# Graph attention on one core: 40 columns of x a group on ScalarE, 12 a group on VectorE

## The chip, the cores and the metric

The kernel runs on one core of a Trainium2 chip. The metric is device time in microseconds (us) for one execution; smaller is better. The engines are named as in the profile: PE (TensorE, with PEld for its weight loads), DVE (VectorE), ACT (ScalarE), POOL (GpSimd) and SP (SyncE). A "q" behind a name (DVEq, ACTq) is that engine's sequencer: register operations, loads of registers and waits on semaphores, which do not count as busy time of the engine.

## The reference

A graph attention layer over N = 12500 nodes and 212500 edges sorted by destination, with D = 128 and 8 heads of 16:

```python
Q, K, V = x @ WQ, x @ WK, x @ WV              # [N, 8, 16] each
Eh = edge_attr @ WE                           # [E, 8, 16]
score = K[src] * Q[dst] / 4 * Eh
score = exp(clip(score.sum(-1, keepdims=True), -5, 5))
wV = segment_sum(V[src] * score, dst)
Z = segment_sum(score, dst)
h = x + wV / (Z + 1e-6)
h = (h - mean(h)) * rsqrt(var(h) + 1e-5) * gamma + beta   # over the nodes
out = layernorm(x + h)                                    # over the features
```

All data are f32. The sources of the edges are random, so K[src] and V[src] have to be fetched row by row.

## The kernel before

The edges are cut into 1661 tiles of 128. Two units of four tiles make a group, and there are 208 groups of eight tiles (the last is smaller). First a table of K and V of all nodes, `kvd`, is made in DRAM (256 f32 a row). Then one long loop goes over the groups. For each tile of a group 128 rows of the table are wanted; an indirect DMA on POOL (`gather`, L272) brings them, one DMA a tile, into the group's buffer `slot`. There are eight such buffers and a ninth from group 6 on, so gathers can run some groups ahead of their use.

Within the loop, group g goes through these steps on DVE, in this order: `products` (L755, twice: K times the product of Q and Eh, which lies in `ps_t`), `scores` (L762, the sum in each head), `clip_exp` (L771 on DVE, then two exponentials on ACT, L772 and L773), `recip`, `turned_onehot`, `both_halves` (L732), `attn` (L809), `message` (L777: V times the exponential), `onehot` for group g+1 (L674, L676, L677). PE makes the products with matrices, the sum over the edges (L793) and the turns; ACT evacuates PSUM.

POOL's gathers are saved in three ways for some groups, which the code calls `apart`: their eighth tile is not gathered by POOL.

- By columns on ACT: `hx` holds x transposed in SBUF (128 x N). `load_cols` reads node numbers into ACT's registers (`TENSOR_LOAD`, L326, from `col_ids`), and `fetch_cols` copies one column of `hx` a time into `xc` (L363), 32 a group, 16 ahead of the exponentials (half 0) and 16 behind them (half 1). When 128 columns stand, `cols_mm` (L371, on PE) multiplies them with `w_kv` into `pair_ps`, and `cols_out` (L375, on ACT) puts the 256 results into the group's `slot`. `col_plan` says which groups: 49 tiles.
- By rows on SP: `fetch_rows` issues 16 DMAs of one row each a group into `byrow`; `rows_out` (L353, on ACT) copies 128 of them into `slot`. `row_plan`: 24 tiles.

The exponentials and `pair_ps` share one PSUM tile, `ps_m`. The order on each engine is that of the code (the schedule is written out by hand), and a gather is also tied to steps of the loop (`pace`).

The loop's middle, in the order of the code before:

```python
fetch_rows(g)
within(products, g); within(denom, g - 2); within(scores, g)
fetch_cols(g, 0)
within(clip_exp, g); within(recip, g - 2); within(turned_onehot, g + 2); within(both_halves, g + 1)
...
within(gather_sum, g - 1); within(eh_mm, g + 2); cols_mm(g); fetch_cols(g, 1)
within(x_out, g - 3); within(q_out, g + 3); within(sums_out, g - 1)
cols_out(g); rows_out(g)
within(eh_out, g + 2); within(q_window, g + 4); load_cols(g + 1)
within(turn_back, g + 1); within(qe_mm, g + 2)
within(attn, g - 2); within(message, g); within(onehot, g + 1)
```

Of the kernel before, what the change touches and what calls it, by code (L numbers as in the profile page):

```python
# [21 lines left out]
G = 8  # L22
U = 4
# [22 lines left out]

LAST = [3, 2]
# [27 lines left out]
def col_plan(sizes):  # L75
    full = sizes.count(U) // 2
    groups, end = [], P
    while FIRST_COL + -(-end // COLS) - 1 + COL_LAG < full:
        groups.append(max(NX, FIRST_COL + -(-end // COLS) - 1 + COL_LAG))
        end += P  # L80
    assert sorted(set(groups)) == groups
    return groups


def row_plan(sizes):
    full, used = sizes.count(U) // 2, set(col_plan(sizes))
    groups, end = [], P
    while True:
        g = FIRST_ROW + -(-end // SP_ROWS) + ROW_LAG
        while g in used:  # L90
            g += 1
        if g >= full:
            return groups
        used.add(g)
        groups.append(g)
        end += P


def row_groups(sizes):
    return [2 * g for g in col_plan(sizes) + row_plan(sizes)]  # L100


@with_exitstack
def gnn_kernel(
# [31 lines left out]
    consts = ctx.enter_context(tc.tile_pool(name="consts", bufs=1))  # L136
# [23 lines left out]
    pair_ps = small_ps[:, 0:2, :].rearrange("p a b -> p (a b)")  # L160
# [91 lines left out]
    KV, XG, SLOT, PAIR = {}, {}, {}, {}  # L252
# [30 lines left out]
    def issue(n=0):  # L283
        while len(queued) > n:
            f, *a = queued.pop(0)
            f(*a)
# [9 lines left out]

    col_tiles = col_plan(usizes)
    tot = len(col_tiles) * P
    assert tot % (2 * COLS) == 0 and tot // (2 * COLS) <= P and P % COLS == COLS % LOAD == 0
# [4 lines left out]
    apart = set(col_tiles + row_tiles)  # L304
    row_ids = consts.tile([P, 2 * SP_ROWS], I32, name="row_ids")
    nc.vector.memset(row_ids, 0)
    rows_in = [tc.alloc_semaphore(f"rows_in{i}") for i in range(NSEM)]
    kvb = kvd.bitcast(U8).rearrange("n d -> (n d)")
    BY_ROW = {}
    XC = {}  # L310

    def load_col_ids():
        n, m = 2 * SP_ROWS, tot_rows // (2 * SP_ROWS)
        nc.sync.dma_start(row_ids[:m], bass.AP(tensor=rsrc.tensor, offset=rsrc.offset + tot, ap=[[n, m], [1, n]]))
        m = tot // (2 * COLS)
        nc.sync.dma_start(col_ids[:m], bass.AP(tensor=rsrc.tensor, offset=rsrc.offset, ap=[[2 * COLS, m], [1, 2 * COLS]]))

    OFFS = {}

    def load_cols(g):  # L320
        q = g - FIRST_COL
        if 0 <= q < tot // COLS:
            OFFS[g] = []
            for c in range(0, COLS, LOAD):
                at = q % 2 * COLS + c
                _, offs = nc.values_load_multi_w_load_instructions(  # L326
                    col_ids[q // 2:q // 2 + 1, at:at + LOAD], engines=(ET.Activation,), min_val=0, max_val=N - 1,
                    skip_runtime_bounds_check_because="node ids")
                OFFS[g] += offs

    def fetch_rows(g):
        q = g - FIRST_ROW
# [6 lines left out]
        for r, off in enumerate(offs, q * SP_ROWS):  # L339
# [16 lines left out]
    def fetch_cols(g, half):  # L356
        if g in OFFS:
            at = (g - FIRST_COL) * COLS
            for c in range(half * COLS // 2, (half + 1) * COLS // 2):
                k, r = col_tiles[(at + c) // P], (at + c) % P  # L360
                if r == 0:
                    XC[k] = late[0].tile([P, P], F32, name="xc", bufs=2)
                nc.scalar.activation(XC[k][:, r:r + 1], hx[:, ds(OFFS[g][c], 1)], AF.Copy)  # L363

    def col_tile(g):
        q = (g - FIRST_COL) * COLS
        return col_tiles[q // P - 1] if q > 0 and q % P == 0 and q <= tot else None

    def cols_mm(g):
        if col_tile(g) is not None:  # L370
            nc.tensor.matmul(pair_ps, XC[col_tile(g)], w_kv, start=True, stop=True)  # L371

    def cols_out(g):
        if col_tile(g) is not None:
            nc.scalar.activation(KV[col_tile(g)](G - 1, G, 0, 2 * P)[:, 0, :], pair_ps, AF.Copy)  # L375

    def load_kv():
        while free and pending and table[0]:
# [54 lines left out]
    def within(f, g):  # L433
        return f(g) if 0 <= g < NG else None
# [458 lines left out]
    for q in range(NQ):  # L893
# [13 lines left out]
        k = q - first_step  # L907
# [64 lines left out]
    for g in range(NG - 2):  # L972
        if g % 2 == 0:
            load(g // 2 + 2)
        within(load_rel, g + 3)
        if (g + 6) % RQ == 0 and (g + 6) // RQ in quads:
            load_quad((g + 6) // RQ)
        fetch_rows(g)
        within(products, g)
        within(denom, g - 2)  # L980
        within(scores, g)
        fetch_cols(g, 0)
        within(clip_exp, g)
# [60 lines left out]
        if g == LATE - 1:  # L1044
            tps.close()
            late.append(tps.enter_context(tc.tile_pool(name="late", bufs=1)))
        if g == LATE - 2:
            free.append(NSLOT)
            load_kv()
    last = NG - 1  # L1050
    g = last - 1
# [3 lines left out]
                           skip_runtime_bounds_check_because="a count")]  # L1055
# [332 lines left out]
```

## Time and profile before

| | before |
|---|---|
| median of 3 runs | 2059.93 us (2055.01 to 2061.22) |
| the profiled execution | 2061.55 us, its span 2059.6 us |
| granted PE clock | 0.951 |
| busy: PE, DVE, POOL, ACT | 1768.6, 1543.5, 1541.2, 1225.2 us |
| gathers of `kvd` by POOL | 1524 |
| bytes by DMA | 379.50 MB, mean 184 GB/s |

The span is from the first to the last instruction; 1.95 us of the execution lie outside it. A row of a group of instructions reads: line, engine, operation, output<-inputs, shape, count, then busy us and mean ns of one, then the idle time of the engine just before them and what ended most of it. In a row of the chronological view the first two numbers are the start and the duration, both in us; what stands in square brackets is the idle time before it. A row of the view of one line gives the shortest, the median and the longest duration in ns, and the first and the last start in us.

### The profile page before, as it was taken

The page shows a single profiled execution, that of the slowest core. Times are in us where ns is not written, and L with a number is a line of the kernel's source. Part 1 is how long each engine was busy: PE and PEld are TensorE (multiplying, and loading weights), DVE is VectorE, ACT ScalarE, POOL GpSimd, SP SyncE. Part 2 cuts the span into 40 slices and gives each one's busy share as a digit, 9 for nine tenths or more (in the row PEclk, how much of TensorE's full clock was granted, in tenths as well). Part 3 has the DMA queues.
Part 4 walks back from the last instruction along what each step waited for, and adds up shares of the span by engine and source line. Part 5 has one row for each costly group of instructions (what it writes and reads, how often), then busy time and mean ns, then how long its engine had stood idle before and what let it go on. Part 6 is the DMA issues. An engine that isn't in the chain of part 4 may idle for free. (4 is left out here: it accounts for less than half of the span.)

```text
span 2059.6 us, 50464 instructions
## 1 busy us (share of the span) xinstructions
PE 1768.6 (86%) x9096; PEld 1121.2 (54%) x9096; DVE 1543.5 (75%) x3157; ACT 1225.2 (59%) x8700; POOL 1541.2 (75%) x1624
## 2 busy tenths in 40 slices
PE   7899999998888888888888888788888878888887
PEld 7676566665554545554554554454555445445556
DVE  4568899987777687777777777677777777777777
ACT  2356677766565565565665666565566566566545
POOL 7677777777777777777777777777777777777775
PEclk9999999999999999999999999999899999999998
DMA  7855556655555555555555555555555555555563
GB/s 266 304 184 180 190 186 195 203 182 188 180 167 185 174 178 175 174 188 170 175 187 166 175 190 161 181 186 175 167 184 174 170 179 184 164 179 184 192 202 127
DMA packets 133493, 379.50 MB, mean 184 GB/s; under 512 B 37631, under 2 KB 50602, under 8 KB 119338
## 3 DMA queue, kind: packets, MB, share of 16 engines
q0 software_dynamic: 75200, 204.05, 32.9%
q1 hardware_dynamic: 54776, 171.01, 23.7%
q14 instruction: 257, 2.11, 0.3%
q10 hardware_dynamic: 3186, 1.13, 0.2%
q8 instruction: 74, 1.21, 0.2%
HBM read 350.60 MB, written 25.44 MB: 183 GB/s over the span
## 5 line engine op out<-in xcount | busy, mean ns | idle before, releaser
L272 POOL DMA_INDIRECT slot<-kvd,srcs x1524 | 1451.5, 952 | 468.5 <-issue 283.5
L363 ACT ACTIVATE xc<-hx 128x1 f32 x6272 | 647.0, 190 | 267.5 <-issue 231.7
L755 DVE TENSOR_TENSOR slot<-slot,ps_t 128x512 f32<-128x512 f32 x410 | 271.4, 680 | 342.6 <-DMA slot<-kvd,srcs 254.8
L793 PE MATMUL ps_a<-msg,oh 128*128 128x136 f32 (+1 forms) x3322 | 519.6, 295 | 2.6 <-DVE msg L777 2.6
L793 PEld LDWEIGHTS ps_a<-msg,oh 128*128 128x128 f32 (+1 forms) x3322 | 419.3, 168 | 81.4 <-issue 52.2
L707 PE MATMUL ps_e<-ea,w_e 128*128 128x512 f32 x832 | 391.0, 592 | 0.1
L740 PE MATMUL ps_t<-ident,wt 128*128 128x128 f32 x1661 | 256.6, 295 | 125.0 <-DVE wt L732 121.6
L740 PEld LDWEIGHTS ps_t<-ident,wt 128*128 128x128 f32 x1661 | 197.7, 149 | 264.0 <-DVE wt L732 221.5
L777 DVE TENSOR_TENSOR msg<-slot,ps_m 128x1024 f32<-128x1024 f32 (+2 forms) x209 | 248.7, 1192 | 65.6 <-ACT slot L375 63.7
L772 ACT ACTIVATE ps_m<-s 128x64 f32<-128x64 f32 (+1 forms) x209 | 47.0, 225 | 399.1 <-DVE s L771 320.3
L732 DVE TENSOR_TENSOR wt<-wt,ps_q 128x512 f32<-128x512 f32 x416 | 264.6, 676 | 2.4 <-PE ps_q L722 2.3
L722 PE MATMUL ps_q<-ot,qs 64*128 64x512 f32 x832 | 264.3, 715 | 0.0
L762 DVE TENSOR_REDUCE s<-slot 128x64 f32<-128x1024 f32 (+1 forms) x208 | 249.8, 1202 | 0.2
L715 ACT ACTIVATE wt<-ps_e 128x512 f32<-128x512 f32 x416 | 231.9, 622 | 9.3 <-PE ps_e L707 9.1
L707 PEld LDWEIGHTS ps_e<-ea,w_e 128*128 128x128 f32 x832 | 143.5, 191 | 100.2 <-issue 98.7
L818 PEld LDWEIGHTS ps_a<-ident,at 128*128 128x128 f32 x408 | 65.9, 203 | 179.9 <-ACT xw L661 69.0
L674 DVE TENSOR_TENSOR oh<-ps_m,rel 128x512 f32<-128x512 f32 x208 | 141.7, 681 | 0.0
L694 PE MATMUL ps_a<-w_q,xw 128*128 128x128 f32 x416 | 95.6, 313 | 31.5 <-ACT xw L661 29.9
L836 ACT ACTIVATE ring<-ps_a 128x64 f32 x408 | 89.6, 220 | 46.7 <-PE ps_a L793 12.4
L818 PE MATMUL ps_a<-ident,at 128*128 128x128 f32 x408 | 106.9, 347 | 10.0 <-ACT os L798 7.0
L661 ACT ACTIVATE xw<-hx 128x64 f32 x416 | 89.1, 285 | 16.0 <-DMA hx<-xT 8.2
L371 PE MATMUL ps_m<-w_kv,xc 128*128 128x256 f32 x98 | 35.6, 447 | 71.7 <-ACT ps_m L772 71.6
(187 smaller groups left out, 1608.9 us busy)
## 6 DMA issues: line engine op xcount, KB each, us to landing
ea<-eaT SPq DMA_DIRECT2D x103, 1024.0 KB
byrow<-kvd SPq DMA_DIRECT2D x3072, 1.0 KB
slot<-kvd,srcs POOLq DMA_INDIRECT x1524
rbq<-relT SPq DMA_DIRECT2D x94, 128.0 KB
kvd<-slot SPq DMA_DIRECT2D x12, 512.0 KB
kvd<-t SPq DMA_DIRECT2D x12, 512.0 KB
ring<-xT SPq DMA_DIRECT2D x24, 256.0 KB
hT<-ring SPq DMA_DIRECT2D x23, 256.0 KB
```

The lines of the kernel that those rows point to most:

```text
L272: return nc.gpsimd.indirect_dma_start(out=out, out_offset=None, in_=table, in_offset=bass.IndirectOffsetOnAxis(ap=part(SRC, e, 1), axis=0))
L363: nc.scalar.activation(XC[k][:, r:r + 1], hx[:, ds(OFFS[g][c], 1)], AF.Copy)
L707: by(("eh", g), nc.tensor.matmul(eh, w_e, EA[g][:, a:b, :].rearrange("p a b -> p (a b)"), start=True, stop=True))
L715: nc.scalar.activation(t[:, :(b - a) * P], EH[g][h], AF.Copy)
L722: by(("qe", g), nc.tensor.matmul(QE[g][h], QS[g][r], OT[g][r, :(b - a) * P], start=True, stop=True))
L732: by(("both", g), nc.vector.tensor_tensor(t, t, QE[g][h], op=OP.mult))
L740: by(("back", g), nc.tensor.transpose(ps[:, j, :], WT[g][h][:, j * P:(j + 1) * P], ident))
L755: step = nc.vector.tensor_tensor(kv, kv, PW[g][i][:, :b - a, :], op=OP.mult)
L762: step = nc.vector.tensor_reduce(SS[g][:, a:b, :], KV[g](a, b, 0).rearrange("p t (h d) -> p t h d", d=DH), axis=AX.X, op=OP.add)
L777: step = nc.vector.tensor_tensor(MSG[g][:, a:b, :P].rearrange("p t (h d) -> p t h d", d=DH), KV[g](a, b, P).rearrange("p t (h d) -> p t h ...
L793: by(("sum", g), nc.tensor.matmul(AGG[g][WN if j >= n else 0:], OH[g][j], MSG[g][:, j, :], start=(j == 0), stop=(j == n - 1)))
L818: nc.tensor.matmul(ps, AT[g], ident, start=True, stop=False)
```

## The change

Three things are changed.

1. ACT fetches 40 columns a group (20 and 20) in place of 32, so `col_plan` finds 61 tiles in place of 49. The load of registers is split: 20 values ahead of `q_window`, 20 behind it.
2. DVE fetches columns too: `load_v(g)` reads 12 node numbers into DVE's registers behind `scores`, and `fetch_v(g)` copies 12 columns of `hx` into `xv` behind `onehot(g + 1)`, in groups 8 to 199. A new plan, `v_plan`, gives these 2304 columns to 18 more tiles, at groups where no other tile's columns are multiplied.
3. `cols_mm` and `cols_out` serve both kinds of tile. POOL gathers 30 tiles fewer: 1494. The 16 rows a group by SP stay as they are, and so do their 24 tiles.

The core of the diff:

```diff
-COLS = 32
-LOAD = 16
+COLS = 40
+LOAD = 20
+V_COLS = 12
+def v_plan(sizes):
+    full, used = sizes.count(U) // 2, set(col_plan(sizes) + row_plan(sizes))
+    tiles, at, end = [], [], P
+    while True:
+        m = FIRST_COL + -(-end // V_COLS)
+        while (m - FIRST_COL) * COLS % P < COLS:
+            m += 1
+        g = m + COL_LAG
+        while g in used:
+            g += 1
+        if g >= full:
+            return tiles, at
+        used.add(g)
+        tiles.append(g)
+        at.append(m)
+        end += P
...
+    def load_v(g):
+        q = g - FIRST_COL
+        if 0 <= q < -(-tot_v // V_COLS):
+            at = q % 2 * V_COLS
+            _, OFFV[g] = nc.values_load_multi_w_load_instructions(
+                v_ids[q // 2:q // 2 + 1, at:at + V_COLS], engines=(ET.DVE,), min_val=0, max_val=N - 1,
+                skip_runtime_bounds_check_because="node ids")
+
+    def fetch_v(g):
+        for r, off in zip(range((g - FIRST_COL) * V_COLS, tot_v), OFFV.get(g, ())):
+            k = r // P
+            if r % P == 0:
+                XV[k] = wp.tile([P, P], F32, name="xv", bufs=2)
+            nc.vector.tensor_copy(XV[k][:, r % P:r % P + 1], hx[:, ds(off, 1)])
...
     def cols_mm(g):
-        if col_tile(g) is not None:
-            nc.tensor.matmul(pair_ps, XC[col_tile(g)], w_kv, start=True, stop=True)
+        t = XC[col_tile(g)] if col_tile(g) is not None else XV[v_at.index(g)] if g in v_at else None
+        if t is not None:
+            nc.tensor.matmul(pair_ps, t, w_kv, start=True, stop=True)
...
         within(scores, g)
+        load_v(g)
         fetch_cols(g, 0)
...
         within(eh_out, g + 2)
+        load_cols(g + 1, 0)
         within(q_window, g + 4)
-        load_cols(g + 1)
+        load_cols(g + 1, 1)
...
         within(onehot, g + 1)
+        fetch_v(g)
```

The lines of the kernel move by this: L755 becomes L803, L762 L810, L771 L819, L777 L825, L677 L725, L363 L384, L371 L418, L375 L423 and L272 L291 in the changed kernel (where L755 is a product on PE). `fetch_v` is L365 there and `load_v` L356.

On DVE one group of the loop before, from the clip of the scores to the next group's products (`slot_...`, `oh`, `ot`, `wt` are tiles of the group):

```order
L771 TENSOR_SCALAR s<-s 128x64
L805 RECIPROCAL rz<-rz 128x8
L684 TENSOR_SCALAR ot<-rbq,wiota 128x512
L732 TENSOR_TENSOR wt<-wt,ps_q 128x512 x2
L809 SCALAR_TENSOR_TENSOR at<-os,keep,rz 128x128
L777 TENSOR_TENSOR msg<-slot_1377,ps_m 128x8x128
L674 TENSOR_TENSOR oh<-ps_m,rel 128x512
L676 TENSOR_SCALAR oh<-rel,lim 128x4
L677 TENSOR_TENSOR oh<-ps_m,rel 128x256
L755 TENSOR_TENSOR slot_1420<-slot_1420,ps_t 128x4x128 x2
```

The same stretch on DVE in the changed kernel (`v_ids` holds the node numbers, `xv` the columns):

```order
L356 TENSOR_LOAD v_ids
L819 TENSOR_SCALAR s<-s 128x64
L853 RECIPROCAL rz<-rz 128x8
L732 TENSOR_SCALAR ot<-rbq,wiota 128x512
L780 TENSOR_TENSOR wt<-wt,ps_q 128x512 x2
L857 SCALAR_TENSOR_TENSOR at<-os,keep,rz 128x128
L825 TENSOR_TENSOR msg<-slot_9864,ps_m 128x8x128
L722 TENSOR_TENSOR oh<-ps_m,rel 128x512
L724 TENSOR_SCALAR oh<-rel,lim 128x4
L725 TENSOR_TENSOR oh<-ps_m,rel 128x256
L365 ISA
L365 COPY xv<-hx 128x1
```

The last two rows stand there twelve times, the ISA being a register operation that makes the address of the copy behind it; only then come the products, L803. The load of the twelve registers stands between the sum L810 and the clip.

On ACT before, from the evacuation of `ps_e` to the first column of the next group (`xw` are windows of `hx`):

```order
L715 ACTIVATE wt<-ps_e 128x512 x2
L661 ISA
L661 ACTIVATE xw<-hx 128x64
L661 ISA
L661 ACTIVATE xw<-hx 128x64
L326 TENSOR_LOAD col_ids x2
L363 ISA
L363 ACTIVATE xc<-hx 128x1
```

The same on ACT in the changed kernel:

```order
L763 ACTIVATE wt<-ps_e 128x512 x2
L373 TENSOR_LOAD col_ids
L709 ISA
L709 ACTIVATE xw<-hx 128x64
L709 ISA
L709 ACTIVATE xw<-hx 128x64
L373 TENSOR_LOAD col_ids
L384 ISA
L384 ACTIVATE xc<-hx 128x1
```

One of the two loads has moved ahead of the windows, behind the evacuations.

More of the change, by code (lines that the diff above doesn't have):

```diff
@@ L298, in gnn_kernel @@
     tot = len(col_tiles) * P
-    assert tot % (2 * COLS) == 0 and tot // (2 * COLS) <= P and P % COLS == COLS % LOAD == 0
+    assert -(-tot // (2 * COLS)) <= P and COLS == 2 * LOAD
     col_ids = consts.tile([P, 2 * COLS], I32, name="col_ids")
@@ L303, in gnn_kernel @@
     assert tot_rows % (2 * SP_ROWS) == 0 and row_tiles == sorted(row_tiles)
-    apart = set(col_tiles + row_tiles)
+    v_tiles, v_at = v_plan(usizes)
+    tot_v = len(v_tiles) * P
+    apart = set(col_tiles + row_tiles + v_tiles)
+    v_ids = consts.tile([P, 2 * V_COLS], I32, name="v_ids")
+    nc.vector.memset(v_ids, 0)
+    XV = {}
     row_ids = consts.tile([P, 2 * SP_ROWS], I32, name="row_ids")
@@ L310, in gnn_kernel, with load_ids @@
     XC = {}
-    def load_col_ids():
[L313 to L316, printed above, removed]
+    nc.vector.memset(col_ids, 0)
+    def load_ids(to, n, first, total):
+        m, rest = divmod(total, n)
+        for p, k, w in ((0, m, n), (m, 1, rest)):
+            if w and k:
+                nc.sync.dma_start(to[p:p + k, :w], bass.AP(
+                    tensor=rsrc.tensor, offset=rsrc.offset + first + n * p, ap=[[n, k], [1, w]]))
@@ new lines, in load_col_ids @@
+    def load_col_ids():
+        load_ids(col_ids, 2 * COLS, 0, tot)
+        load_ids(row_ids, 2 * SP_ROWS, tot, tot_rows)
+        load_ids(v_ids, 2 * V_COLS, tot + tot_rows, tot_v)
+    OFFV = {}
+    def load_v(g):
[5 more added lines that the diff above has]
+                skip_runtime_bounds_check_because="node ids")
@@ L318, in gnn_kernel, with load_cols @@
+    def fetch_v(g):
[4 more added lines that the diff above has]
+            nc.vector.tensor_copy(XV[k][:, r % P:r % P + 1], hx[:, ds(off, 1)])
     OFFS = {}
-    def load_cols(g):
+    def load_cols(g, half):
         q = g - FIRST_COL
[L322 to L329, printed above, removed]
+        if 0 <= q < -(-tot // COLS):
+            at = q % 2 * COLS + half * LOAD
+            _, offs = nc.values_load_multi_w_load_instructions(
+                col_ids[q // 2:q // 2 + 1, at:at + LOAD], engines=(ET.Activation,), min_val=0, max_val=N - 1,
+                skip_runtime_bounds_check_because="node ids")
+            OFFS[g, half] = offs
@@ new lines, in fetch_cols, with col_tile @@
+    def fetch_cols(g, half):
+        first = (g - FIRST_COL) * COLS + half * LOAD
+        for r, off in zip(range(first, tot), OFFS.get((g, half), ())):
+            k = col_tiles[r // P]
+            if r % P == 0:
+                XC[k] = late[0].tile([P, P], F32, name="xc", bufs=2)
+            nc.scalar.activation(XC[k][:, r % P:r % P + 1], hx[:, ds(off, 1)], AF.Copy)
+    def col_tile(g):
+        q = (g - FIRST_COL) * COLS
+        return col_tiles[q // P - 1] if 0 < q // P <= len(col_tiles) and q % P < COLS else None
@@ L354, in rows_out @@
             tc.declare_no_dep(step.ins, group=f"rows{k}", reason="the semaphore of the rows")
[L356 to L367, printed above, removed]
     def cols_mm(g):
-        if col_tile(g) is not None:
-            nc.tensor.matmul(pair_ps, XC[col_tile(g)], w_kv, start=True, stop=True)
+        t = XC[col_tile(g)] if col_tile(g) is not None else XV[v_at.index(g)] if g in v_at else None
+        if t is not None:
+            nc.tensor.matmul(pair_ps, t, w_kv, start=True, stop=True)
     def cols_out(g):
-        if col_tile(g) is not None:
-            nc.scalar.activation(KV[col_tile(g)](G - 1, G, 0, 2 * P)[:, 0, :], pair_ps, AF.Copy)
+        k = col_tile(g) if col_tile(g) is not None else v_tiles[v_at.index(g)] if g in v_at else None
+        if k is not None:
+            nc.scalar.activation(KV[k](G - 1, G, 0, 2 * P)[:, 0, :], pair_ps, AF.Copy)
     def load_kv():
```

2 lines of the change are left out of this document (1 added, 1 removed).

## The prediction

> **What bounds the kernel now.** I began with the page: the engines' shares, then the costliest groups with the idle time ahead of them.
>
> ```profile
> L272 POOL DMA_INDIRECT slot<-kvd,srcs x1524 | 1451.5, 952 | 468.5 <-issue 283.5
> L363 ACT ACTIVATE xc<-hx 128x1 f32 x6272 | 647.0, 190 | 267.5 <-issue 231.7
> L755 DVE TENSOR_TENSOR slot<-slot,ps_t 128x512 f32<-128x512 f32 x410 | 271.4, 680 | 342.6 <-DMA slot<-kvd,srcs 254.8
> L772 ACT ACTIVATE ps_m<-s 128x64 f32<-128x64 f32 (+1 forms) x209 | 47.0, 225 | 399.1 <-DVE s L771 320.3
> ```
>
> DVE stands 342.6 us ahead of its products, mostly until a gather has landed. So the next view is that of the line of the gathers, with the first and the last start.
>
> ```profile
> L272 POOL DMA_INDIRECT slot<-kvd,srcs x1524: 942/946/1223, 88.4 to 2003.1; - x191
> ```
>
> 1523 steps in 2003.1 - 88.4 = 1914.7 us are 1.257 us each, and a gather's 0.952 us with its share of idle time, 468.5 / 1524 = 0.31, is the same: POOL issues without a pause from 88.4 us to the end. The other side is DVE's own pace, which shows only where gathers are ahead of it. The groups of DVE in two stretches, 162 to 452 us and 452 to 1990 us:
>
> ```profile
> L755 DVE TENSOR_TENSOR slot<-slot,ps_t 128x512 f32<-128x512 f32 x74 | 47.2, 679 | 3.2 <-PE ps_t L740 3.2
> L777 DVE TENSOR_TENSOR msg<-slot,ps_m 128x1024 f32<-128x1024 f32 x36 | 43.7, 1215 | 19.1 <-ACT slot L375 19.0
> ...
> L755 DVE TENSOR_TENSOR slot<-slot,ps_t 128x512 f32<-128x512 f32 x322 | 215.4, 681 | 328.8 <-DMA slot<-kvd,srcs 252.8 <-PE ps_e L707 39.1 <-PE ps_a L793 21.6
> ```
>
> In the first stretch DVE waits for no gather (3.2 us); POOL had a start: from 88.4 us to 162 it issued 58 gathers, seven groups. In the second it has caught up and waits 328.8 us (the PE lines named had long been done; I count all of it as gathers). A free group looks like this in order of time:
>
> ```profile
> 349.71 1.22 DVE L762 TENSOR_REDUCE s<-slot 128x64 f32<-128x1024 f32 x1
> 350.96 0.20 DVE L771 TENSOR_SCALAR s<-s 128x64 f32<-128x64 f32 x1
> 351.07 0.19 DVE L805 RECIPROCAL rz<-rz 128x8 f32<-128x8 f32 x1
> 351.19 0.43 DVE L684 TENSOR_SCALAR ot<-rbq,wiota 128x512 f32<-128x512 uint8 x1
> ...
> 354.85 0.23 DVE L676 TENSOR_SCALAR oh<-rel,lim 128x4 f32<-128x4 f32 x1
> 354.98 0.42 DVE L677 TENSOR_TENSOR oh<-ps_m,rel 128x256 f32<-128x256 f32 x1
> 355.32 1.27 DVE L755 TENSOR_TENSOR slot<-slot,ps_t 128x512 f32<-128x512 f32 x2
> 356.51 0.25 DVE L802 TENSOR_SCALAR rz<-os 128x8 f32<-128x8 f32 x1
> 356.63 1.22 DVE L762 TENSOR_REDUCE s<-slot 128x64 f32<-128x1024 f32 x1
> ```
>
> 356.63 - 349.71 = 6.92 us with no gap: DVE is the second bound, close behind POOL. So there are two clocks. POOL's ends where its gathers end; DVE's is its own work, and 328.8 us is all that can be put on DVE before it sets the time.
>
> **POOL's side.** 30 gathers fewer are 30 x 1.257 = 37.7 us. What lies ahead of the first gather and behind the last stays. If nothing else came to count, the span would be 2059.6 - 37.7 = 2021.9 us. That is the floor.
>
> **The copies on DVE.** They stand behind L677 and ahead of the products: in the free state on the path, in the waiting state inside the wait. The trace of before has no column copied by DVE; its nearest are ACT's columns and DVE's own small instructions. ACT's run of 16:
>
> ```profile
> 358.11 0.23 ACT L772 ACTIVATE ps_m<-s 128x64 f32<-128x64 f32 x1
> 358.27 0.24 ACT L773 ACTIVATE msg<-s 128x64 f32<-128x64 f32 x1
> 358.42 1.58 ACT L363 ACTIVATE xc<-hx 128x1 f32 x16
> ...
> 360.89 0.39 ACT L375 ACTIVATE slot<-ps_m 128x256 f32<-128x256 f32 x1 [0.20 <-PE ps_m L371]
> ...
> 364.07 1.67 ACT L363 ACTIVATE xc<-hx 128x1 f32 x16 [1.53 <-issue]
> ```
>
> Less the last one's 0.19 us, 15 steps take 1.67 - 0.19 = 1.48 us: 0.099 us for a register step and its column, though one column lasts 0.19. A column's pace is thus the sequencer's. How DVE's sequencer compares shows in what both do alike, their waits on semaphores (DVE's, then ACT's at two lines) and the load of a register:
>
> ```profile
> L755 DVEq EVENT_SEMAPHORE  x802: 21/50/6601, 113.9 to 2007.9; - x161
> ...
> L836 ACTq EVENT_SEMAPHORE  x129: 17/17/391, 117.5 to 2014.6; - x129
> ...
> L375 ACTq EVENT_SEMAPHORE  x192: 38/38/38, 237.1 to 1984.7; - x192
> ...
> L326 ACTq TENSOR_LOAD <-col_ids x392: 1006/1047/1851, 166.3 to 1967.6; - x196
> ...
> L654 ACTq TENSOR_LOAD <-base_i x104: 307/312/1286, 37.3 to 1965.6; - x104
> ...
> L1054 ACTq TENSOR_LOAD <-bad_i x1: 287/287/287, 1993.2 to 1993.2; - x1
> ...
> L1054 DVEq TENSOR_LOAD <-bad_i x1: 543/543/543, 1996.2 to 1996.2; - x1
> ```
>
> 21 against 17 ns and 50 against 38 make DVE's steps 1.24 to 1.32 times as long, so a register step and a copy should take 0.099 x 1.27 = 0.126 us, twelve 1.51 us. Two waits on semaphores for the products come behind them, 0.05 us each, hidden today; and the sequencer has a start, since it works on the first copies while L677 runs (354.98 to 355.32, 0.34 us). 1.51 + 0.10 - 0.34 = 1.27, and 0.06 for copies that meet POOL at the port: L802 lasts 166 ns at the median and 190 in the mean, 24 ns more by a few long ones, and most of that falls into the sequencer's gaps.
>
> ```profile
> L802 DVE TENSOR_SCALAR rz<-os x208: 155/166/417, 104.7 to 2013.1; 128x8 f32<-128x8 f32 x104
> ...
> L802 DVE TENSOR_SCALAR rz<-os 128x8 f32<-128x8 f32 x208 | 39.4, 190 | 5.0 <-ACT os L798 4.9
> ```
>
> So 1.33 us a group, in 192 groups 255 us. The ends: from below ACT's own pace with the same start, 1.19 - 0.34 = 0.85; from above one copy at a time, 12 x 0.166 = 2.0 or, with a register step of 0.037 between, 2.4. I take 1.33 since ACT's row is the same operation, and 1.6 (no start) as the high end of the range.
>
> **The load of twelve registers.** By ACT's rows 4 values take 0.312 us and 16 take 1.047, 0.061 for each more; one value takes 0.543 us on DVE against 0.287 on ACT. So 0.543 + 11 x 0.061 = 1.21 us, beginning with L762, which lasts 1.22 us and hides it. If all of the load is longer by that ratio, (0.312 + 8 x 0.061) x 543 / 287 = 1.51, and 0.29 sticks out. Between 0 and 0.29 I take 0.08, near the first, 15 us in all.
>
> **The waits for a finished tile.** At a group where columns are multiplied, `message` waits for ACT's L375, as both use `ps_m`:
>
> ```profile
> 361.31 1.22 DVE L777 TENSOR_TENSOR msg<-slot,ps_m 128x1024 f32<-128x1024 f32 x1 [1.32 <-ACT slot L375]
> ...
> DVE msg L777 <- ACT slot L375: 63.7, 48, 5.7
> ```
>
> 63.7 / 48 = 1.33 us each. ACT's chain from the exponential (358.11) to L375 holds the second half of the columns, now 20 in place of 16: 4 x 0.099 = 0.40 longer. 61 + 18 = 79 tiles by 1.73 are 137 us, 73 more than today. If only the chain without delays counts (1.2 + 0.4), it is 63 more; at 2.0, 94 more.
>
> **What is hidden.** ACT gets 8 columns (0.79 us), longer loads (20 values by the same slope 1.29 us, the first now under the evacuations; some 0.25 us more exposed) and 30 x 0.40 us of L375: 1.1 us a group. Its wait for the clipped scores, 399.1 us over 208 groups, 1.9 each, covers that; were it gone, the exponential would be late and a group longer by up to those 1.1 us. PE gets 30 more products of two passes at 0.447 us, 27 us, in groups where it waits for DVE. SP's queue has the same rows, and two or three more loads of ids at group 2. Slots: DVE stays behind the gathers, so POOL's lead holds.
>
> **The sum.** DVE gets 255 + 15 + 73 = 343 us and has 328.8 us of waits to put them into: span 2059.6 + 343 - 328.8 = 2073.8 us, with the 1.95 us outside the span 2075.8; I say 2075 us. That the profiled execution (2061.55) is 1.6 us over the median counts for nothing here. POOL's 37.7 us are lost, as POOL ends up waiting. The point where the sum gives no change is 328.8 us, copies of 1.26 us a group; the floor is reached at 291 us, copies of 1.06.
>
> **The rivals.** First, copies cheap enough that gathers still set the end. For it speaks that small DVE instructions without register follow one another by 0.11 us (350.96, 351.07), 12 x 0.11 - 0.34 = 0.98 us: then 188 + 15 + 73 = 276, under 291, and the time is the floor, 2021.9 + 1.95 = 2024 us. Against it stand the slower register steps. The Trainium skill, Vector Engine (DVE) Microarchitecture Reference, 5.2 Measured stream behaviour on trn2, gives some 75 ns for each DVE instruction in a queue; by that rule, which no row here shows, the copies would take at most 0.9 us and the floor would be the time.
>
> Second, copies that do not overlap: if the register step waits for the copy ahead of it, 2.4 us a group, 461 + 15 + 73 = 549, span 2059.6 + 220 = 2280. It decides from 1.26 us on. ACT's columns, which overlap, speak against it.
>
> Third, the copies slow POOL. The longest gather lasts 1223 ns against a median of 946, 0.28 us more. A run of 1.33 us meets 1.06 gathers; at 0.28 each that is 192 x 0.30 = 57 us on POOL's chain, span 2079, time 2081, whatever DVE does. Against it: the mean is 952, 6 ns over the median, although L684, a copy-like instruction in SBUF of 0.43 us, runs every group. The Trainium skill, SBUF — State Buffer, SBUF: two separate sides, says that an f32 copy from SBUF to SBUF on VectorE locks GpSimd out of writing descriptors; how far that holds for one element a partition no run here shows yet.
>
> That the change doesn't do what it says I exclude, as the program holds 30 gathers fewer.
>
> **Chances.** Forecast case 0.62, the first rival 0.24, the second 0.08, the third 0.06. Within the forecast case the sum is uncertain by some 40 us, so it gives 0.12 to faster, 0.10 to the same and 0.40 to slower. About 0.3%, 6 us, is what a measurement can tell from no change. Faster 0.24 + 0.12 = 0.36, same 0.10, slower 0.40 + 0.08 + 0.06 = 0.54. The range reaches from the floor with 2 us to spare, 2022, to copies of 1.6 us with a load that sticks out by 0.2: 192 x 1.8 + 73 = 419, span 2150. The second rival is left out.
>
> **What would show it.** Right: copies about 0.126 us apart; DVE's wait ahead of the products under 60 us; 79 waits of `message` of about 1.7 us; POOL with gaps, 1494 gathers over more than 1880 us. If POOL still issues every 1.26 us to the end and the span is near 2022, the copies or the waits were cheaper than I made them. A mean gather over 1.0 us would speak for the third rival, copies 0.2 us apart for the second.

## The result and the profile after

| | before | after |
|---|---|---|
| median of 4 runs | 2060.36 us (2055.01 to 2061.22) | 2033.24 us (2031.59 to 2036.56) |
| ratio to before | | 0.9873, 95% interval 0.9854 to 0.9892 |
| the profiled execution's span | 2059.6 us | 2034.7 us |
| busy: DVE, POOL, ACT | 1543.5, 1541.2, 1225.2 us | 1741.5, 1510.8, 1398.8 us |

The kernel became 27 us faster where 15 us slower was forecast. These are the groups of the page that answer to those shown of before, and behind them the row of `message`, first of before and then of after (busy us and mean ns, then idle time ahead and what ended most of it):

```profile
L291 POOL DMA_INDIRECT slot<-kvd,srcs x1494 | 1421.3, 951 | 459.5 <-issue 264.4
L384 ACT ACTIVATE xc<-hx 128x1 f32 x7808 | 796.1, 190 | 262.5 <-issue 232.0
L803 DVE TENSOR_TENSOR slot<-slot,ps_t 128x512 f32<-128x512 f32 x410 | 262.4, 681 | 23.0 <-PE ps_t L788 8.4
L820 ACT ACTIVATE ps_m<-s 128x64 f32<-128x64 f32 (+1 forms) x209 | 46.2, 221 | 158.9 <-DVE s L819 115.6
...
L777 DVE TENSOR_TENSOR msg<-slot,ps_m 128x1024 f32<-128x1024 f32 (+2 forms) x209 | 248.7, 1192 | 65.6 <-ACT slot L375 63.7
...
L825 DVE TENSOR_TENSOR msg<-slot,ps_m 128x1024 f32<-128x1024 f32 (+2 forms) x209 | 248.7, 1191 | 161.9 <-ACT slot L423 161.2
```

DVE's idle time ahead of the products went from 342.6 us to 23.0, and its waits for a gather are all but gone. In their place stand 161.9 us ahead of `message`. That is how it looks when DVE is the bound, as the forecast said, only less late than forecast; the experiments below test it. The same as a sum: DVE's busy time grew by 1741.5 - 1543.5 = 198.0 us, its idle time ahead of `message` by 161.9 - 65.6 = 96.3, and that ahead of the products fell by 319.6; together -25 us, and the span fell by 24.9.

The line of the gathers (shortest, median and longest duration in ns, first and last start in us) shows what POOL did meanwhile:

```profile
L291 POOL DMA_INDIRECT slot<-kvd,srcs x1494: 942/946/1212, 88.2 to 1963.5; - x187
```

1493 steps in 1875.3 us are 1.256 us each: POOL still issued without a pause, and its last gather starts 39.6 us sooner than before. So POOL did not wait for DVE, which I had forecast. The granted PE clock rose from 0.951 to 0.981, but a step of the gathers took 1.257 us before and takes 1.256 now, so the clock does not explain the gain. From POOL's last start to the end of the span are now 71.2 us, where before they were 56.5: DVE ended 15 us further behind the gathers than before, about one and a half groups of eight gathers, and the nine buffers took up that much.

What a copy costs is seen in the view in order of time, where a row of x12 goes from the first copy's start to the last one's end, and in that of its line. The two rows below that of x12 are the first five and the last four of the same twelve:

```profile
355.10 0.41 DVE L725 TENSOR_TENSOR oh<-ps_m,rel 128x256 f32<-128x256 f32 x1
355.44 1.05 DVE L365 COPY xv<-hx 128x1 f32 x12
...
355.44 0.38 DVE L365 COPY xv<-hx 128x1 f32 x5
...
355.99 0.50 DVE L365 COPY xv<-hx 128x1 f32 x4
...
356.57 1.28 DVE L803 TENSOR_TENSOR slot<-slot,ps_t 128x512 f32<-128x512 f32 x2
...
L365 DVEq FUSED_REGOPS  x2304: 46/46/46, 172.6 to 1922.6; - x192
L365 DVE COPY xv<-hx x2304: 133/145/156, 173.1 to 1922.7; 128x1 f32 x192
...
L365 DVE COPY xv<-hx 128x1 f32 x2304 | 207.4, 147 | 5.5 <-issue 5.0
...
L356 DVEq TENSOR_LOAD <-v_ids x192: 845/868/1104, 167.5 to 1916.2; - x192
```

From the start of L725 to that of the products are 1.47 us, where before they were 0.34: twelve copies cost 1.13 us, forecast 1.33. The first five start (0.38 - 0.14) / 4 = 0.06 us apart, the last four (0.50 - 0.154) / 3 = 0.115, where 0.14 and 0.154 us are the last copy's own time: the sequencer's register steps (FUSED_REGOPS) run ahead of the first copies, until that start is used up. The load of twelve registers takes 0.868 us and lies wholly under the sum, which lasts 1.22.

### The profile page after: what moved, and what is told of

The parts are those of the page before. It is cut to its first block, busy times and chain, and to the rows that moved or that the text cites. A ratio compares the mean times of both kernels' runs of the same rounds, so it can differ in the third digit from the quotient of the medians.

```text
span 2034.7 us, 58507 instructions
## 1 busy us (share of the span) xinstructions
PE 1739.2 (85%) x9156; PEld 1109.5 (55%) x9156; DVE 1741.5 (86%) x5463; ACT 1398.8 (69%) x10266; POOL 1510.8 (74%) x1594
## 3 DMA queue, kind: packets, MB, share of 16 engines
q10 hardware_dynamic: 3186, 1.13, 0.2%
## 5 line engine op out<-in xcount | busy, mean ns | idle before, releaser
L291 POOL DMA_INDIRECT slot<-kvd,srcs x1494 | 1421.3, 951 | 459.5 <-issue 264.4
L384 ACT ACTIVATE xc<-hx 128x1 f32 x7808 | 796.1, 190 | 262.5 <-issue 232.0
L755 PE MATMUL ps_e<-ea,w_e 128*128 128x512 f32 x832 | 390.8, 592 | 0.1
L825 DVE TENSOR_TENSOR msg<-slot,ps_m 128x1024 f32<-128x1024 f32 (+2 forms) x209 | 248.7, 1191 | 161.9 <-ACT slot L423 161.2
L788 PE MATMUL ps_t<-ident,wt 128*128 128x128 f32 x1661 | 236.1, 279 | 67.8 <-DVE wt L780 65.3
L788 PEld LDWEIGHTS ps_t<-ident,wt 128*128 128x128 f32 x1661 | 185.1, 140 | 186.4 <-DVE wt L780 159.0
L803 DVE TENSOR_TENSOR slot<-slot,ps_t 128x512 f32<-128x512 f32 x410 | 262.4, 681 | 23.0 <-PE ps_t L788 8.4
L810 DVE TENSOR_REDUCE s<-slot 128x64 f32<-128x1024 f32 (+1 forms) x208 | 249.8, 1202 | 0.2
L770 PE MATMUL ps_q<-ot,qs 64*128 64x512 f32 x832 | 235.6, 643 | 0.0
L365 DVE COPY xv<-hx 128x1 f32 x2304 | 207.4, 147 | 5.5 <-issue 5.0
L755 PEld LDWEIGHTS ps_e<-ea,w_e 128*128 128x128 f32 x832 | 143.3, 190 | 100.1 <-issue 98.6
L742 PEld LDWEIGHTS ps_a<-w_q,xw 128*128 128x128 f32 x416 | 63.8, 193 | 187.7 <-ACT xw L709 184.7
L820 ACT ACTIVATE ps_m<-s 128x64 f32<-128x64 f32 (+1 forms) x209 | 46.2, 221 | 158.9 <-DVE s L819 115.6
L709 ACT ACTIVATE xw<-hx 128x64 f32 x416 | 83.6, 249 | 70.2 <-issue 53.4
L866 PE MATMUL ps_a<-ident,at 128*128 128x128 f32 x408 | 101.1, 330 | 20.2 <-ACT os L846 15.4
```

What stands on the lines that cost most here:

```text
L291: return nc.gpsimd.indirect_dma_start(out=out, out_offset=None, in_=table, in_offset=bass.IndirectOffsetOnAxis(ap=part(SRC, e, 1), axis=0))
L365: nc.vector.tensor_copy(XV[k][:, r % P:r % P + 1], hx[:, ds(off, 1)])
L384: nc.scalar.activation(XC[k][:, r % P:r % P + 1], hx[:, ds(off, 1)], AF.Copy)
L755: by(("eh", g), nc.tensor.matmul(eh, w_e, EA[g][:, a:b, :].rearrange("p a b -> p (a b)"), start=True, stop=True))
L770: by(("qe", g), nc.tensor.matmul(QE[g][h], QS[g][r], OT[g][r, :(b - a) * P], start=True, stop=True))
L788: by(("back", g), nc.tensor.transpose(ps[:, j, :], WT[g][h][:, j * P:(j + 1) * P], ident))
```

## The experiments

Two theories were at odds. Theory 1: DVE's own work, copies and waits for ACT among it, sets the end of the changed kernel, some 10 us above the floor, the 2024 us that POOL's 1494 gathers allow by the forecast. Theory 2: the gathers still set it.

In twelve of the eighteen runs all kernels, that of before among them, took some 2720 us or more, and the traces show long stalls in ACT's register steps; two chips showed this at one time and not at another. They are told last. The six runs that follow stand beside runs of before at 2060 to 2064 us. A row of the view of waits gives who waited, for whom, then the us in total, the times and the longest in us.

**More copies (i1).** The changed kernel with

```diff
-V_COLS = 12
+V_COLS = 16
```

> Once more the changed kernel with 16 of VectorE's columns in place of 12, for a run in which ScalarE's sequencer does not stall. Theory 1 (VectorE sets the end): 768 more copies of .1145 us on an engine without waits for gathers left, about 2033 + 88 = 2121 us, somewhat more if more of the products wait for the reload of the message. Theory 2 (the gathers still set the end): 6 fewer at 1.257 us, 2025 us.

Measured: 2125.54 us, ratio to before 1.031 (1.0293 to 1.0327). DVE's wait ahead of `message`, in the changed kernel and in this run, then the line of the gathers:

```profile
DVE msg L825 <- ACT slot L423: 161.2, 79, 4.9
...
DVE msg L825 <- ACT slot L423: 155.4, 85, 3.8
...
L291 POOL DMA_INDIRECT slot<-kvd,srcs x1488: 941/947/1212, 89.3 to 2010.8; - x186
```

The span grew by 2123.4 - 2034.7 = 88.7 us for 768 copies: 0.1155 us each, nothing hidden, though POOL has six gathers fewer. And now POOL does pause: 1921.5 us over 1487 steps are 1.292 each. Theory 2 is out for 16 copies; for 12 the next run decides. From the changed kernel on, one more copy a group costs 22 us.

**No copies (j1).** The changed kernel with the copies replaced by one `memset` of the tile (the kernel leaves out the fetched values, so these rows of keys and values are wrong):

```diff
-            nc.vector.tensor_copy(XV[k][:, r % P:r % P + 1], hx[:, ds(off, 1)])
+            if r % P == 0:
+                nc.vector.memset(XV[k], 0.0)
```

> The changed kernel without VectorE's 2304 copies, for a run in which ScalarE's sequencer does not stall (the twelve columns are set to zero once per ring, so these rows of keys and values are wrong). Theory 1 (VectorE sets the end of the changed kernel): without 217 us of copies the gathers set it, at 1.257 us without gaps: 2024 us, VectorE waiting for gathers by over 100 us. Theory 2 (the gathers set the end already): 2033 us.

Measured: 2021.29 us, ratio 0.9815 (0.9799 to 0.9831), span 2018.7. DVE's waits and the gathers (one line is added, so L825 is L826 and L803 is L804):

```profile
DVE msg L826 <- ACT slot L424: 191.2, 78, 4.9
DVE slot L804 <- DMA slot<-kvd,srcs: 123.7, 59, 6.4
...
L291 POOL DMA_INDIRECT slot<-kvd,srcs x1494: 942/946/1217, 88.6 to 1964.5; - x187
```

The gathers run as in the changed kernel, the last starting at 1964.5 us in place of 1963.5, but the end follows 54.2 us later and not 71.2. Theory 2 had 2033 us for this run, so it is out for 12 copies too. So the copies' whole effect on the end of the changed kernel is what DVE lags behind, about 12 us by the medians, of the 217 us (192 x 1.13) that they take. The waits of `message` are there without any copy, and even longer, 2.45 us each against 161.2 / 79 = 2.04.

**ScalarE's half alone (k1).** `v_plan` gives no tiles:

```diff
 def v_plan(sizes):
+    return [], []
```

> ScalarE's half alone, for a run in which ScalarE's sequencer does not stall: 40 columns for ScalarE, none for VectorE, 12 of the 30 gathers gone. The gathers set the end: 2060 - 12 x 1.257 = 2045 us; so VectorE's half brings the changed kernel the other 12 us, of the 22.6 that its 18 gathers take. The rival, that ScalarE's longer lists hold up the products' other operands by themselves (the waits of the message's product for its reload come from ScalarE's half): 2055 us or above, and these waits above 120 us in the trace.

Measured: 2044.97 us, ratio 0.9915 (0.9899 to 0.9932), as both theories had it.

```profile
DVE slot L804 <- DMA slot<-kvd,srcs: 204.4, 80, 5.6
DVE msg L826 <- ACT slot L424: 149.1, 61, 4.4
...
ACT ps_m L821 <- DVE s L820: 146.6, 82, 5.0
```

The waits of `message` are 149.1 / 61 = 2.44 us each, against 1.33 before: it is ScalarE's half, the 8 more columns a group with their longer loads, that makes them longer by 1.1 us. VectorE's half makes them more numerous, 79, and each shorter, 2.04. Here they cost nothing, since DVE has 204.4 us of waits for gathers left.

The last row shows where the 1.1 us come from: ACT's exponential waited for the clipped scores 82 times, where before it was 133 times (some more waits, 16 and 28, are put down to DVE's reciprocal behind the clip):

```profile
ACT ps_m L772 <- DVE s L771: 320.3, 133, 7.1
```

In the other groups ACT comes to the exponential late. Over the groups with a column tile, the traces of the loop give a mean of 0.11 us from the clip's end to the exponential's start before, and of 0.78 here; from there to the end of ACT's copy into `slot` (L375, L424) it is 3.10 us before and 3.56 here. So 0.46 us of the longer wait are the longer chain and 0.67 the late start. The rival had coupled the long waits to 2055 us or more; the waits came, the time did not. So ScalarE's half brings 15 to 17 us, VectorE's half 12, of the 22.6 that its 18 gathers are worth at 1.257 us.

**Cheaper copies (j2).** The same 2304 copies from a column that stands in the code (the kernel leaves out the choice of the column, so these rows of keys and values are wrong):

```diff
-            nc.vector.tensor_copy(XV[k][:, r % P:r % P + 1], hx[:, ds(off, 1)])
+            nc.vector.tensor_copy(XV[k][:, r % P:r % P + 1], hx[:, r:r + 1])
```

> The changed kernel with its 2304 copies from columns that stand in the code (the copy's own number) in place of columns named by a register, so these rows of keys and values are wrong; number, form and order of the copies are the same, only the register steps on VectorE's queue are gone. Theory 1 (a copy is paced by VectorE's sequencer at .1145 us, .046 us of it the register step, and VectorE sets the end): the copies follow one another at about .060 us as the queued ones do, a group's cost 12 x .060 = .7 us in place of 1.13, VectorE gains 192 x .4 = 80 us and the gathers set the end: 2024 us. The rival (a copy costs by its own 133 to 156 ns, whatever names its column): 2033 us and no change in the pace.

Measured: 2028.68 us, ratio 0.984 (0.9823 to 0.9856), span 2026.1. Order of time, then the copies' line, DVE's wait and the gathers:

```profile
350.93 0.42 DVE L725 TENSOR_TENSOR oh<-ps_m,rel 128x256 f32<-128x256 f32 x1
351.27 0.81 DVE L365 COPY xv<-hx 128x1 f32<-128x1 f32 x12
351.99 0.68 DVE L803 TENSOR_TENSOR slot<-slot,ps_t 128x512 f32<-128x512 f32 x1
...
L365 DVE COPY xv<-hx x2304: 134/143/148, 174.6 to 1912.2; 128x1 f32<-128x1 f32 x192
...
DVE slot L803 <- DMA slot<-kvd,srcs: 45.5, 23, 3.6
...
L291 POOL DMA_INDIRECT slot<-kvd,srcs x1494: 942/947/1212, 89.8 to 1971.2; - x187
```

A copy lasts as long as in the changed kernel (143 ns at the median, 145 there), but twelve take 0.81 us in place of 1.05, all 0.06 us apart, and the products start 1.06 us after L725 in place of 1.47. So the register step sets the pace of the later copies, and it costs DVE 0.41 us a group. The time fell by 4.6 us and not to the floor: DVE waits for gathers again, 45.5 us, and the end follows the last gather by 54.9 us, so it is the gathers that set the end. These are 7.7 us later than in the changed kernel, with 1881.4 / 1493 = 1.260 us a step. Their mean is 955 ns here against 951, and four ns by 1494 are 6 us. Whether the copies cost the gathers those 4 ns, or it is this run, was not tried; `i3` below, with register-named copies, has the same 955.

**The waits moved away (g1, i3).** The column tile's product and its evacuation go ahead of the group's products, so that ACT fills `slot` before the exponentials and not behind them:

```diff
         fetch_rows(g)
+        cols_mm(g)
         within(products, g)
...
         fetch_cols(g, 0)
+        cols_out(g)
         within(clip_exp, g)
...
-        cols_mm(g)
         fetch_cols(g, 1)
...
-        cols_out(g)
         rows_out(g)
```

> The changed kernel with cols_mm and cols_out moved ahead of the exponentials of their group (cols_mm to the group's start, cols_out between the first half of the columns and the exponentials), so that message has nothing of ps_m to wait for. Theory 1 (VectorE's work, waits of message among it, sets the end): 161 us of waits go, VectorE falls below POOL, and POOL sets the end: span 2021.9, time 2024 us, POOL without gaps, and some 100 to 150 us of VectorE's waits for gathers come back. Theory 2 (POOL sets the end already): 2033 us, no change. Where register steps of ScalarE take 0.7 us at times, the gain would be less or more than this and is read against the runs of the kernel before beside it.

Measured: 2021.61 us, ratio 0.9801 (0.9784 to 0.9817). DVE's rows of the page:

```profile
L803 DVE TENSOR_TENSOR slot<-slot,ps_t 128x512 f32<-128x512 f32 x410 | 268.3, 682 | 163.1 <-DMA slot<-kvd,srcs 125.7
L825 DVE TENSOR_TENSOR msg<-slot,ps_m 128x1024 f32<-128x1024 f32 (+2 forms) x209 | 247.9, 1188 | 4.2 <-ACT ps_m L820 3.4
```

The 161.9 us ahead of `message` are 4.2, and the waits for gathers are back. With all copies in it, the kernel runs as fast as the one without copies: the other way to free DVE from what it lags behind. Then four copies more, in this order:

> Once more the kernel with the column tile's matmul and its stores to the ring moved ahead of the products, and 16 columns for VectorE, for a run in which ScalarE's sequencer does not stall. In the run with 12 columns in this order (2022 us) VectorE had 125.7 us of waits for gathers left and none for the message's reload. Theory 1: 88 us more of copies fit into these, the gathers still set the end, 6 fewer at 1.257 us: 2014 us, with about 38 us of VectorE's waits for gathers left. The rival: the copies take run-ahead of the products too and VectorE sets the end: 2022 to 2035 us.

Measured: 2018.13 us, ratio 0.9792 (0.9775 to 0.9808).

```profile
L803 DVE TENSOR_TENSOR slot<-slot,ps_t 128x512 f32<-128x512 f32 x410 | 265.4, 682 | 70.4 <-DMA slot<-kvd,srcs 41.3
...
L291 POOL DMA_INDIRECT slot<-kvd,srcs x1488: 942/946/1203, 89.8 to 1963.2; - x186
```

125.7 - 41.3 = 84 us of waits went into 768 copies, as forecast (88), and the end did not move back: what cost 92 us in the changed kernel's order is free in this one. Both beat the kernel before and the changed one. 2014 us were expected: between this run and the one before it the intervals overlap, so the last six gathers' worth is not shown; here too the gathers took 955 ns in the mean and 1.260 us a step.

**The runs with stalls.** There the kernel before took 2754 to 2804 us. The first of them had each part alone (`e2` is the changed kernel with COLS = 32 and LOAD = 16, so VectorE's half alone; `e1`, `e3` and `e4` are the edits shown above for no VectorE tiles, no copies and 16 copies).

> ScalarE's part alone: 40 columns a group, no column by VectorE (61 + 24 tiles spared, 1512 gathers). Theory 1 (in the changed kernel VectorE's own work sets the end, before it POOL's gathers did): here VectorE gets only longer waits of message (61 x 2.0 against 64 us), POOL sets the end, span 2059.6 - 12 x 1.257 = 2044.5, time 2046 us; DVE still waits over 200 us ahead of its products. Theory 2 (POOL's gathers set the end in all of them, the copies lie in the waits): 2046 us as well. If the 8 columns more on ScalarE cost anything, the time is above 2050.

> VectorE's part alone: 32 columns a group by ScalarE as before, 12 by VectorE (49 + 24 + 18 tiles spared, 1506 gathers). Theory 1: VectorE's work is that of the changed kernel less the waits of message for 12 tiles and with shorter ones (67 x 1.6 = 107 in place of 161 us), so 2034.7 - 54 = 1981 us, below POOL's 2059.6 - 18 x 1.257 = 2037.0; POOL sets the end, time 2039 us. Theory 2: 2039 too. A third reading, that copies on VectorE cost time one for one wherever they stand, gives 2046 + 217 = over 2200.

> The changed kernel with VectorE's copies of columns left out (the 18 tiles are zeroed once instead, so their rows are not the right ones); gathers, loads of registers, products and waits stay. Theory 1: 217 us of VectorE's work are gone, POOL sets the end: span 2021.9, time 2024 us, and DVE waits some 180 us for gathers. Theory 2 (POOL sets the end already): as the changed kernel, 2033.

> 16 columns a group by VectorE in place of 12 (24 tiles, 1488 gathers). Theory 1: 192 x 4 x 0.1145 = 88 us more on VectorE and 6 waits of message of 2.0 us: 2033 + 100 = 2133 us, with gaps in POOL. Theory 2: 6 gathers fewer, 2033 - 8 = 2025 us.

Measured, as ratios to before: e1 0.9883 (0.9846 to 0.992), e2 1.0015 (0.9985 to 1.0045), e3 0.9882 (0.9848 to 0.9917), e4 0.9919 (0.9892 to 0.9945). No theory gives this. ACT's columns in the run of 8 more columns alone, here and in the run of 2044.97 us (the same kernel):

```profile
L385 ACTq FUSED_REGOPS  x7808: 3/37/1377, 245.8 to 2640.4; - x196
...
L385 ACTq FUSED_REGOPS  x7808: 37/37/37, 168.3 to 1958.1; - x196
```

A register step, always 37 ns in the second, takes up to 1377 in the first; 624 of the 7808 are longer than 60 ns, and what they have too much adds up to 376 us, of the 678 by which the span is longer. So these steps are not all of it: in the first 165 us, before any column is fetched, POOL began 40 gathers of `kvd` in e1 and 61 in k1. DVE's waits are then mostly for ACT (in e4 `message` waits 327.2 us for L423 alone), and the copies fall into them: e4, whose kernel is 104 us above that of e3 elsewhere, is 11 us above it here. So these runs say nothing on which of DVE and POOL sets the end of the changed kernel. The same edits fell into the stalls three more times. With 16 copies and with none:

> The kernel with 16 columns a group by VectorE once more, for a place where the kernel before takes its 2060 us. Theory 1 (VectorE's work sets the end): about 100 us over the changed kernel, 2133 us, with gaps in POOL. Theory 2 (POOL's gathers set the end): 6 gathers fewer, 2025 us. If the register steps take 0.7 us at times here too, the run says nothing on either.

> The changed kernel with VectorE's copies left out (the 18 tiles are zeroed once instead, so their rows are not the right ones), once more. Theory 1: POOL sets the end again, span 2021.9, time 2024 us, with some 180 us of VectorE's waits for gathers. Theory 2: as the changed kernel, 2033 us.

Measured, as ratios to before: 0.9902 (0.9876 to 0.9928) and 0.9866 (0.9837 to 0.9896). Then with 16 copies, with none, with 40 columns alone, and 16 copies in the early order:

> The changed kernel with 16 of VectorE's columns in place of 12 (6 more gathers gone). Theory 1 (VectorE's own work, its copies and its waits for the message's reload, sets the end of the changed kernel): 768 more copies at a sequencer's pace of .1145 us add 88 us to an engine that has only 1.7 us of waits for gathers left, so about 2033 + 88 = 2121 us, somewhat more if more of the products wait for the reload. Theory 2 (the gathers still set the end): 6 fewer at 1.257 us, 2033 - 8 = 2025 us.

> The changed kernel without VectorE's 2304 copies: the twelve columns are set to zero once per ring in place of being copied, so these rows of keys and values are wrong and all else runs. Theory 1 (VectorE sets the end): without 217 us of copies the gathers set it again, without gaps at 1.257 us: the floor of 2022 us of span, about 2024 us, and VectorE waits for gathers by over 100 us again. Theory 2 (the gathers set the end already): 2033 us, as with the copies.

> ScalarE's half alone: 40 columns for ScalarE in place of 32, none for VectorE, so 12 of the 30 gathers go. Both theories: the gathers set the end, 2060 - 12 x 1.257 = 2045 us, since ScalarE has more than its 8 x 192 x .0975 = 150 us to spare; a third, that ScalarE's longer lists hold up the products' other operands, would give 2055 to 2065 us.

> The changed kernel with the column tile's matmul and its stores to the ring moved ahead of the products (as in the run that gave 2022 us), and 16 columns for VectorE. In that run VectorE had 125.7 us of waits for gathers left and none for the message's reload. Theory 1: 88 us more of copies fit into these, so the gathers still set the end, 6 fewer: 2022 - 7.5 = 2014 us, with about 38 us of waits left. The rival: the copies take run-ahead of the products too, and VectorE sets the end: 2022 to 2035 us.

Measured, as ratios to before: 0.986 (0.9828 to 0.9892), 0.9856 (0.9804 to 0.9907), 0.9868 (0.9829 to 0.9907) and 0.9849 (0.9812 to 0.9886): four kernels that lie up to 107 us apart elsewhere, the same here. And without copies once more:

> Once more the changed kernel without VectorE's 2304 copies (the twelve columns are set to zero once per ring and these rows of keys and values are wrong), for a run in which ScalarE's sequencer does not stall. Theory 1 (VectorE sets the end of the changed kernel): without 217 us of copies the gathers set the end, at 1.257 us without gaps: 2024 us, and VectorE waits for gathers by over 100 us. Theory 2 (the gathers set the end already): 2033 us.

Measured, as a ratio to before: 0.9856 (0.9825 to 0.9888); the same kernel took 2021.29 us (j1) on the same chip some time later.

One kernel ran only there, the early order with 16 copies and

```diff
-COLS = 40
-LOAD = 20
+COLS = 44
+LOAD = 22
```

> The column tile's matmul and its stores ahead of the products, 16 columns for VectorE and 44 for ScalarE (22 a load): 6 gathers fewer than in the run with 16 and 40 (2018 us, VectorE's waits for gathers 41 us, ScalarE idle in several hundred us). Theory 1: the gathers set the end where VectorE has waits left: 2018 - 6 x 1.257 = 2010.6 us, with 41 - 7.5 = 34 us of waits left. The rival: ScalarE's 192 x 4 x .0975 = 75 us more hold up the scores' exponentials or the reload of the message: 2018 us or above, with waits of VectorE for ScalarE in the trace.

Measured: ratio 1.1281 (1.1252 to 1.131). `message` waits 720.4 us for ACT's exponentials there. Such waits were the rival's sign, but with 40 columns in the same order and the same stalls (h4) they are 352.3 us already, so the run does not decide for the rival:

```profile
DVE msg L825 <- ACT ps_m L820: 720.4, 141, 7.2
```

What 44 columns do where ACT does not stall stays open, and so does the reason of the stalls. The granted clock was lower as well (0.832 in e1 against 0.974 in k1); whether that is a cause or a consequence is not shown.

## Why the prediction was wrong

The mechanism held: VectorE's half exchanges POOL's time for DVE's, and DVE ends as the bound (i1, j1 and g1 show it from three sides). What failed is the sizes in the sum, most of all the price of the copies and the load. The sum put 343 us on DVE against 328.8 of waits, so the sign hung on 14 us, 4% of the sum, while the forecast time was off by 42 us.

- **The copies**, 255 us forecast, are 217 by the free group (192 x 1.13). The step that failed is the ratio of DVE's sequencer to ACT's, 1.27, taken from waits on semaphores. In i1 a further copy costs 0.1155 us, where I had 0.126; ACT's pace in the row of the prediction is 0.099, so the ratio is 1.17. The ratio held for the register step alone, 46 ns against 37 or 1.24, but not for the rest of a copy's step. The 0.06 us for the port was not there either: 12 x 0.1155 - 0.34 + 0.10 = 1.15, and 1.13 was measured, so the run-ahead under L725 and the waits behind the copies were about right together. The first rival had taken small instructions without a register as the price; copies without one do follow each other as closely as that and closer (j2), but these have one. The second rival fell too: it had copies 0.2 us apart, and they overlap. The 75 ns of the Trainium skill's Vector Engine (DVE) Microarchitecture Reference, 5.2 Measured stream behaviour on trn2, agree roughly with j2's 60 ns, but a copy whose column a register names took 115 where the sequencer's start was used up.
- **The load of registers**, 15 us forecast, is 0: 0.868 us under 1.22.
- **The waits of `message`**, 73 us more forecast, are 97: 79 of 2.04 us where I had 1.73. The step that failed is that the rest of ACT's new work is hidden under its wait for the scores. The second half of the columns, 0.40 us by the forecast, made the chain 0.46 us longer in k1, about as forecast; the other 0.67 us there are ACT's late start. ACT's idle time ahead of the exponential did shrink, from 399.1 us to 158.9, but it is not there in every group. Where DVE is slower still, in i1, ACT is hardly late (0.12 us in the mean), and the wait of `message` is 155.4 / 85 = 1.83 us, near the forecast.
- **DVE's busy time** grew by 198.0 us where copies and load had 270. By the page's rows the copies hold 207.4 us of it, and the products fell from 271.4 to 262.4 at the same mean: 207.4 - 9.0 = 198.4. The rest of the copies' 217 us is the gap behind the last copy, from 355.44 + 1.05 to 356.57, which counts as idle time ahead of the products. Why the products' row fell is not shown; instructions of DVE that follow without a gap overlap (355.10 + 0.41 is later than 355.44), the overlap counts once, and there are fewer gaps now.
- **What is left over** ahead of the products is 23.0 us, where the forecast had 342.6 - 328.8 = 13.8; some 10 of it are those gaps behind the copies. So -72 for DVE's busy time, +24 for `message` and +9 here make the 39 us between the forecast span, 2073.8, and the measured 2034.7.
- **POOL's gaps**, named as the sign of DVE being the bound, are a sign that comes late: when DVE lags by some 12 us the buffers hide them, at 100 (i1) they show.
- **The port.** The third rival, the copies slowing POOL, fell: the mean gather is 951 ns against 952. The Trainium skill, SBUF — State Buffer, SBUF: two separate sides, has VectorE's f32 copy lock GpSimd out of writing descriptors; 2304 copies of one element a partition did not do so to any extent that shows here, and the 4 ns a gather of j2 and i3 are the most that could be its work.

Break-even and floor were placed in one unit, us of DVE's time, and that served; but each term had a single value. At copies of 1.13 us with the other two terms as forecast the sum is 305 us, and the span 2036. That it lies so near the measured 2034.7 is luck: the load (15 us less than forecast), `message` (24 more) and the products' row (9 less) cancel. With the three terms as measured, 217 + 0 + 97 = 314, the span is 2044.8. So most of the 0.54 for slower rested on 0.2 us a group that no row of before could tell.

## What to carry to other kernels

When work is moved from the bound to an engine with waits, count how much it has left after every term, and treat a sum that comes as near to that as the terms are uncertain as open (here 14 us away, with an error of 39); the price of the smallest repeated step decides, and a ratio between engines should come from the same kind of step. Then look for waits of the receiving engine that have nothing to do with the moved work: moving one product and its evacuation ahead took 158 us of waits off DVE and made the copies free. A bound that is late by less than the buffers hold shows no gaps in the other engine's steps: here it showed in the time from POOL's last gather to the end, 71.2 us against 54.2 without the copies.

## What the runs showed of the hardware

A register step lasts 46 ns on DVE and 37 on ACT (changed kernel; k1). A copy of one column named by a register follows the last in 0.06 us on DVE while the register steps have a start, and in 0.115 after that (changed kernel, i1); without a register it is 0.06 for all twelve (j2). In some runs ACT's register steps took up to 1377 ns in place of 37 (e1), and the kernels were a third slower; two chips that showed such stalls (f1 and f2, i2) were free of them later (j2, j1).
